# Four layers over a graph on one core: how layer 0 divides its keys, and a third buffer for turned blocks

## The chip, the cores and the metric

The kernel runs on one core of one Trainium2 chip. What counts is the device time of one execution in microseconds (us). A core has a matrix engine (PE, with a separate queue PEld that loads its weights), a vector engine (DVE), a scalar engine (ACT), GpSimd (POOL) and a queue that mainly issues transfers (SP). Each engine runs its own instructions in order, and waits on semaphores for the others. SBUF is the memory that the engines work in, PSUM holds what PE has computed, in banks of 128 partitions x 512 fp32 numbers.

## The reference

Four graph layers follow each other on 2,708 nodes with 512 features. Each adds its result to its input and normalises the rows. The change is in layer 0, attention of 8 heads with 64 features each:

```python
adj = jnp.maximum(adjacency_matrix, jnp.eye(n))
keys    = jnp.einsum('nj,hjk->hnk', node_matrix, Wks)
queries = jnp.einsum('nj,hjk->hnk', node_matrix, Wqs)
values  = jnp.einsum('nj,hjk->hnk', node_matrix, Wvs)
atts = jnp.einsum('hqk,hmk->hqm', queries, keys) / key_dim ** 0.5
atts = atts - 1e+16 * (1.0 - adj)[None, :, :]
atts = jax.nn.softmax(atts, axis=-1)
return jnp.einsum('hqm,hmk,hko->qo', atts, values, Wo)
...
x = _layernorm(x + _L0_gnn_ref(x, adj, ...))
x = _layernorm(x + _L1_gnn_ref(x, adj, ...))
x = _layernorm(x + _L2_gnn_ref(x, adj, ...))
x = _layernorm(x + _L3_gnn_ref(x, adj, ...))
```

So each head makes a 2708 x 2708 matrix of weights: scores, plus a mask from the adjacency matrix, exponentials of score minus row maximum, and their sums. All is in fp32.

## The kernel before

**Stages.** A first stage (0 to 216 us) computes keys (`KT`), queries (stored to DRAM) and values (`V`). The stage of the change (216 to about 1230 us) is the attention. Then come the output projection and layers 1 to 3, which the change does not touch.

**Pairs and rounds.** The 2,708 queries are 22 chunks of 128 rows (the last, `LAST`, has 20). Two heads are worked on together, so that a `Pair(c, p)` is chunk c with heads 2p and 2p+1; there are 21 x 4 of them, and one `Last` that holds all eight heads of the 20 rows: 85 in all. The loop at the end of the stage works on three pairs in each round: `new` gets its scores, `cur` (of the round before) has its weights turned, `late` (of two rounds before) is multiplied with the values. The order on PE, DVE and ACT is the order of the program, written out by hand (`manual_schedule`).

**What a round does.** For `new`, PE multiplies keys and queries into PSUM banks (L419, from a ring of 7 banks, `ps_s`), one bank for each head and part. DVE reads each bank, adds the mask, writes the score to the tile `s` in SBUF and keeps the maximum of the row (L441, followed by a short instruction that reads the accumulator). From the maxima DVE makes `nm` (L454). ACT then replaces scores by exponentials in place and keeps their sums (L460).

**Keys in two halves.** The 22 chunks of keys are divided into two halves: 0 to 10 (1,408 keys) and 11 to 21 (1,300 keys). Each half has its own tile `s` (tags `s0`, `s1`, two buffers each, `[128, 2 heads, keys]`) and is scored in three parts (`PARTS = 3`): 469, 469, 470 keys, then 433, 433, 434. ACT takes the exponentials of the first half at the end of the round (`weights(0)`) and those of the second half at the start of the next (`weights(1)`).

**Turning.** To multiply with the values, the weights must stand with the keys on the partitions. The first eight chunks of each half are *dealt* (`DEALT = 8`): DVE transposes blocks of 32 x 32 (`blocks`, L466) from `s` into a tile `d` (`dp`, 2 buffers of 1 MB), and four transfers of 256 KB (`deal`, L475, on SP's queue) move `d` into a tile `e` (`ep`, 3 buffers), which PE reads. The other six chunks (`turned`: 8, 9, 10, 19, 20, 21) are transposed whole by PE (L492) into three PSUM banks, which ACT copies to SBUF (L498, L495, L496). The second half of `cur` is transposed in one instruction for both heads, the first half of `new` in two, one for each head (`blocks(0, slice(j, j + 1))`), so that the first can start when the first head's exponentials are there. A `d` buffer is free again when the four transfers that read it have landed; with two buffers, the second half's blocks go to the buffer of the second half of the round before, and the first half's to that of the first half.

**The order of a round on each engine.**
- PE: scores of `new` (L419), values of `late` (L511), transposes of `cur` (L492).
- DVE: twelve instructions L441 of `new`, `nm` (L454), `blocks(1)` of `cur`, `blocks(0)` of `new` (L466).
- ACT: `weights(1)` of `cur` (L460), the preparation of the next chunk's mask, `weights(0)` of `new` (L460), the copy of the finished values (L529), the copies of the turned banks (L498, L495, L496).
- SP: the loads of the next chunk's adjacency rows (L177, L185), then the transfers L475 of `cur` and `new`.

**Preparing the mask.** In three of four rounds a third of the next chunk's adjacency rows (1,024, 1,024 or 660 columns) is prepared: ACT sums the row (`row_sums`, L195), DVE sets the diagonal where it lies in this third (`loops`, L209, in 20 rounds of the loop), ACT scales the rows to a mask (`mask`, L215). In the program `row_sums` stands after the scores of the first half, `loops` and `mask` after the first part of the second half. So DVE does L209 after eight of its twelve instructions L441.

Of the kernel before, what the change touches and what calls it, by code (L numbers as in the profile page):

```python
# [8 lines left out]
F32 = mybir.dt.float32  # L9
# [6 lines left out]
P = 128  # L16
# [6 lines left out]
def kernel(  # L23
# [27 lines left out]
    NC = (N + P - 1) // P  # L51
# [6 lines left out]
    def cols(b):  # L58
        return b * BLK, min(BLK, N - b * BLK)

    def chunks_of(b):
        n0, w = cols(b)
        return [n0 // P + i for i in range((w + P - 1) // P)]

    const = ctx.enter_context(tc.tile_pool(name="const", bufs=1))
    small = ctx.enter_context(tc.tile_pool(name="small", bufs=4))
# [51 lines left out]
    ends = [0, 8, 16, NC]  # L118
    KD4 = P // 32
    HALVES = 2  # L120
    PARTS = 3
    DEALT = 8
    bounds = [0, NC // 2, NC]

    def dealt(c):
        return any(a <= c < a + DEALT for a in bounds[:-1])
# [19 lines left out]
    with ExitStack() as l0:  # L146
# [40 lines left out]
        def row_sums(c, k):  # L187

            r0, q = rows(c)
            a = loaded[c][0]  # L190
            n0, w = batch(k)
            dst = dgp[:, c, k : k + 1]
            if c == LAST:
                q, dst = 32, dgz[:, k : k + 1]
            nc.scalar.activation(a[:q, n0 : n0 + w], a[:q, n0 : n0 + w], AF.Copy, accum_out=dst[:q])  # L195
            if c == LAST and k == NW - 1:
                nc.sync.dma_start(dgp[:LR, c, :], dgz[FILL:32, :])
# [13 lines left out]
        def mask(c, k):  # L211

            n0, w = batch(k)
            a = loaded[c][0][:, n0 : n0 + w]
            nc.scalar.activation(a, a, AF.Identity, scale=1e16, bias=far)  # L215

        with tc.tile_pool(name="kvw", bufs=1) as kvw, tc.tile_pool(name="xTb", bufs=2) as xtp, tc.tile_pool(
            name="ps_0", bufs=8, space=PSUM
# [63 lines left out]
            for b in order:  # L282
                n0, w = cols(b)
# [100 lines left out]
        ps_a = l0.enter_context(tc.tile_pool(name="ps_a", bufs=1, space=PSUM, reuse_waits="tile"))  # L384
        ps_s = l0.enter_context(tc.tile_pool(name="ps_s", bufs=7, space=PSUM, reuse_waits="tile"))
        sp = l0.enter_context(tc.tile_pool(name="sp", bufs=2, reuse_waits="tile"))
        dp = l0.enter_context(tc.tile_pool(name="dp", bufs=2, reuse_waits="tile"))
        ep = l0.enter_context(tc.tile_pool(name="ep", bufs=3, reuse_waits="tile"))
        ptp = l0.enter_context(tc.tile_pool(name="ptp", bufs=1, reuse_waits="tile"))

        def half(k):

            n0 = bounds[k] * P
            return n0, min(bounds[k + 1] * P, N) - n0

        def bank(shape, name):
            return ps_s.tile(shape, F32, tag="s", name=name)
# [3 lines left out]
        class Pair:  # L401


            def __init__(self, c, p):
                self.c, self.p = c, p
                self.s = []
                self.mx = small.tile([P, 2, HALVES * PARTS], F32, tag="mx", name=f"mx{c}_{p}")
                self.D = {}
                self.E = {}
                self.pts = {}  # L410
                self.done = 0
                self.av = None
# [15 lines left out]
            def scores(self, k, part):  # L428

                c, p = self.c, self.p  # L430
                a = loaded[c][0]
                n0, w = half(k)
                if part == 0:
                    self.s.append(sp.tile([P, 2, w], F32, tag=f"s{k}", name=f"s{c}_{p}_{k}"))
                s = self.s[k]
                h0, h1 = (w * i // PARTS for i in (part, part + 1))
                col = k * PARTS + part
                pss = [bank([P, BLK], f"pss{c}_{p}_{col}_{j}") for j in range(2)]
                self.products(pss, n0 + h0, h1 - h0)
                for j in range(2):  # L440
                    nc.vector.tensor_tensor_reduce(  # L441
                        out=s[:, j, h0:h1],
                        in0=pss[j][:, : h1 - h0],
                        in1=a[:, n0 + h0 : n0 + h1],
                        scale=1.0,
                        scalar=LOW,
                        op0=ALU.add,
                        op1=ALU.max,
                        accum_out=self.mx[:, j, col : col + 1],
                    )  # L450
# [8 lines left out]
                    s = self.s[k][:, j, :]  # L459
                    nc.scalar.activation(s, s, AF.Exp, bias=self.nm[:, j : j + 1], accum_out=self.sums(j, k))  # L460

            def blocks(self, k, heads=slice(0, 2)):

                if k not in self.D:
                    self.D[k] = dp.tile([P, KD4, 2, DEALT, 32], F32, tag="d", name=f"d{self.c}_{self.p}_{k}")
                nc.vector.transpose(  # L466
                    self.D[k].rearrange("p i j m x -> p j m i x")[:, heads],
                    self.s[k][:, heads, : DEALT * P].rearrange("p j (m i x) -> p j m i x", i=KD4, x=32),
                )

            def deal(self, k):
# [139 lines left out]
        with tc.manual_schedule(  # L611
            engines={mybir.EngineType.PE, mybir.EngineType.DVE, mybir.EngineType.Activation}
        ):
            for i in range(len(items) + 2):
                new = None
                more = i < len(items) and items[i][0] < LAST - 1
                prep = more and items[i][1] > 0
                if cur is not None:
                    cur.weights(1)
                if i < len(items):  # L620
                    c, p = items[i]
                    if more:
                        load_chunk(c + 1, p)
                    new = (Pair if c < LAST else Last)(c, p)
                    for part in range(PARTS):
                        new.scores(0, part)
                    if prep:
                        row_sums(c + 1, p - 1)
                    new.scores(1, 0)
                    if prep:  # L630
                        loops(c + 1, p - 1)
                        mask(c + 1, p - 1)
                    for part in range(1, PARTS):
                        new.scores(1, part)
                    new.maxima()
                    new.weights(0)
                if i in (HALF0 * NP + 2, len(items)):
                    sums = heads_sums(i == len(items))
                if late is not None:
                    late.values()  # L640
                if cur is not None:
                    cur.blocks(1)
                    cur.deal(1)
                if new is not None:
                    for j in range(2):
                        new.blocks(0, slice(j, j + 1))
                    new.deal(0)
                if cur is not None:
                    cur.turn()
                if i in (HALF0 * NP + 3, len(items) + 1):  # L650
                    heads_rows(*sums)
                if i == NP:
                    last_sums()
                late, cur = cur, new
# [83 lines left out]
    with tc.tile_pool(name="wo", bufs=1, reuse_waits="tile") as wop:  # L738
        wo_sb = wop.tile([P, KC, D], F32, tag="wo", name="wo_sb")
        load_rows(wo_sb, wo)  # L740
        for c in range(NC):
# [5 lines left out]
            heads = rz_d if c == LAST else rs_d[c >= HALF0][c % HALF0]  # L747
            heads = heads.rearrange("j p q -> j (p q)")
# [129 lines left out]
    if True:  # L878
# [115 lines left out]
        for b in range(NB):  # L994
            for m, _ in enumerate(graph1(b)):
# [6 lines left out]
                if b == NB - 2 and m in (3, 7, 11, 15):  # L1002
                    c = first[(m - 3) // 4]
                    top0(c, 0, piece(c, 0))
                if b == NB - 1 and m < len(first):
                    c = first[m]
# [79 lines left out]
    if True:  # L1086
# [53 lines left out]
        for b in range(NB):  # L1140
            if b:
                queue = Maxima(b + 1) if b + 1 < NB else None
            for m in graph2(b):
                if m % 4 == 2 and 0 <= m // 4 < len(chunks_of(b)) and b:
                    c = chunks_of(b)[m // 4]
# [25 lines left out]
    with tc.tile_pool(name="zp", bufs=2) as zp:  # L1171
# [87 lines left out]
        w = cols(TAIL)[1]  # L1259
# [22 lines left out]
        while n0 < NH * P:  # L1282
            w = min(BLK, NH * P - n0)
            n1 = NH * P + n0
            nchunks = w // P
            j = n0 // BLK
# [102 lines left out]
```

## Time and profile before

| what | value |
|---|---|
| time of three runs | 2588.0, 2579.19, 2587.2 us; median 2587.2 |
| the profiled execution | 2581.24 us; its span 2579.4 us, mean granted PE clock 0.993 |
| first stage, 0 to 216 us | PE busy 211.2, DVE 122.2, ACT 35.5 us |
| attention, 216 to 1230 us | PE busy 1002.5, DVE 967.2, ACT 745.7 us; DMA engines 77% busy, 214 GB/s |
| output projection, 1230 to 1400 us, with the start of layer 1 | PE busy 154.0, DVE 99.7 us |
| layers 1 to 3, 1400 to 2579 us | PE busy 1141.1, DVE 773.2, ACT 348.3 us |
| `nm` (L454), 85 times | first at 216.7 us, last at 1216.6 us |

The span runs from the first to the last instruction. An engine is busy while one of its instructions runs. The ends of PE's matmuls are modelled, so that a PE that is busy for 100% need not be at its limit. In the lines of instructions there stand the line of the program, the engine, the operation, output and input by the program's names, their shapes, how often, the busy time in us, the mean duration of one in ns, and after the last bar how long the engine stood idle just before them, with what ended that idle time.

### The profile page before, as it was taken

To read this page: it belongs to the slowest core of one execution; us is meant where nothing else is said; L and a number is where in the kernel's file an instruction comes from. 1 tells how busy PE (TensorE), PEld (TensorE's weight loads), DVE (VectorE), ACT (ScalarE), POOL (GpSimd) and SP (SyncE) were. 2 spreads that over 40 slices of the span, in tenths; PEclk is the share of its full clock that TensorE was granted. 3 is DMA by queue.
4 is the path that set the end of the run, shared out by engine and by line. 5 is a ranking of instruction groups with operands and counts; after the bars stand their busy time and mean duration, and the time that the engine had idled before them with its cause. 6 is when DMAs were issued, how large, how long until landed. Compare 5 with 4: busy or idle time off the path is not lost. (4 is left out here: it accounts for less than half of the span.)

```text
span 2579.4 us, 42415 instructions
## 1 busy us (share of the span) xinstructions
PE 2508.7 (97%) x15551; PEld 1558.2 (60%) x15551; DVE 1962.2 (76%) x4541; ACT 1154.0 (45%) x2070; POOL 315.7 (12%) x322
## 2 busy tenths in 40 slices
PE   9998999999999999999899999899999999999997
PEld 4886777777777777777456444444444465444465
DVE  3668999999999999999574777988776874543544
ACT  3104778777777777776011001565665640000000
POOL 2110000000000000000210000243332430000000
PEclk9999999999999999999999999999999999999999
DMA  5114787877877777877853444354433213644633
GB/s 167 62 50 138 218 226 211 240 213 220 230 210 219 218 211 215 225 204 186 236 169 94 126 121 142 118 158 138 125 109 116 64 31 114 184 141 143 178 103 105
DMA packets 221498, 411.43 MB, mean 160 GB/s; under 512 B 28765, under 2 KB 48911, under 8 KB 221292
## 3 DMA queue, kind: packets, MB, share of 16 engines
q1 hardware_dynamic: 215052, 392.00, 53.4%
q0 software_dynamic: 6240, 16.73, 1.9%
q8 instruction: 123, 2.02, 0.3%
q14 instruction: 83, 0.68, 0.1%
HBM read 213.55 MB, written 16.72 MB: 89 GB/s over the span
## 5 line engine op out<-in xcount | busy, mean ns | idle before, releaser
L460 ACT ACTIVATE s<-s,nm 128x1408 f32<-128x1408 f32 (+1 forms) x340 | 481.1, 1416 | 244.3 <-DVE nm L454 244.3
L441 DVE CUSTOM_DVE_ANT_0 s<-pss,adj 128x469 f32<-128x469 f32 (+2 forms) x1020 | 565.8, 622 | 8.2 <-PE pss L419 7.0
L419 PE MATMUL pss<-KT,qt 64*128 64x469 f32 (+2 forms) x2016 | 463.7, 561 | 7.2 <-DVE mx L441 4.6
L466 DVE STREAM_TRANSPOSE d<-s 128x1024 f32<-128x1024 f32 (+1 forms) x255 | 393.7, 1580 | 31.6 <-DMA e<-d 16.1
L419 PEld LDWEIGHTS pss<-KT,qt 64*128 64x128 f32 x2016 | 230.1, 187 | 200.3 <-issue 110.8
L811 PE MATMUL acc<-pt,x 128*128 128x512 f32 (+1 forms) x880 | 333.4, 537 | 12.2 <-ACT pt L864 9.7
L511 PE MATMUL av<-e,V 128*64 128x128 f32 x5376 | 309.6, 273 | 4.7 <-DMA e<-d 4.7
L511 PEld LDWEIGHTS av<-e,V 128*64 128x64 f32 x5376 | 297.8, 137 | 5.1 <-issue 5.1
L811 PEld LDWEIGHTS acc<-pt,x 128*128 128x128 f32 x880 | 157.2, 191 | 188.1 <-issue 162.2
L917 PE MATMUL acc<-at,h 128*128 128x512 f32 (+1 forms) x504 | 196.8, 543 | 0.0
L875 POOL TENSOR_TENSOR cs<-cs,pt 128x512 f32<-128x512 f32 (+2 forms) x110 | 157.3, 1430 | 202.7 <-ACT pt L864 200.4
L862 DVE TENSOR_TENSOR pt<-pt,at 128x512 f32<-128x512 f32 (+2 forms) x132 | 107.3, 820 | 75.6 <-ACT pt L861 75.4
L530 POOL DMA_DIRECT2D otd<-ot x84 | 45.2, 538 | 941.7 <-ACT ot L529 921.4
L94 ACT ACTIVATE ln_t<-lnve 128x1 f32<-128x1 f32 x88 | 17.7, 201 | 313.2 <-DVE lnve L108 313.1
L1251 ACT ACTIVATE z<-pz,rdeg 128x512 f32<-128x512 f32 (+1 forms) x22 | 15.1, 688 | 310.9 <-PE pz L823 310.9
L917 PEld LDWEIGHTS acc<-at,h 128*128 128x128 f32 x504 | 90.2, 190 | 101.4 <-issue 99.2
L492 PE MATMUL pst<-ident,s 128*128 128x128 f32 x1020 | 130.0, 277 | 0.0
L864 ACT ACTIVATE pt<-pt 128x512 f32<-128x512 f32 (+2 forms) x132 | 76.1, 579 | 110.0 <-DVE pt L863 109.8
L511 PEld LDWEIGHTS av<-pt,V 128*64 128x64 f32 x1680 | 90.0, 136 | 52.3 <-issue 51.5
L928 DVE SCALAR_TENSOR_TENSOR cs<-at,rdeg,cs 128x512 f32<-128x512 f32 (+2 forms) x126 | 86.2, 684 | 43.7 <-DMA at<-in_adjT_dram 42.4
L492 PEld LDWEIGHTS pst<-ident,s 128*128 128x128 f32 x1020 | 104.2, 133 | 16.8 <-issue 15.1
L511 PE MATMUL av<-pt,V 128*64 128x128 f32 x1680 | 110.3, 278 | 0.2 <-ACT pt L498 0.2
(348 smaller groups left out, 3474.5 us busy)
## 6 DMA issues: line engine op xcount, KB each, us to landing
e<-d SPq DMA_DIRECT2D x680, 256.0 KB
at<-in_adjT_dram SPq DMA_DIRECT2D x210, 256.0 KB
a<-in_adj_dram SPq DMA_DIRECT2D x38, 677.0 KB
adj<-in_adj_dram SPq DMA_DIRECT2D x42, 512.0 KB
at_a<-in_adjT_dram SPq DMA_DIRECT2D x40, 256.0 KB
at_c<-in_adjT_dram SPq DMA_DIRECT2D x40, 256.0 KB
at_f<-in_adjT_dram SPq DMA_DIRECT2D x40, 256.0 KB
adj<-in_adj_dram SPq DMA_DIRECT2D x21, 330.0 KB
```

The costliest lines, as they stand in the source:

```text
L419: nc.tensor.matmul(pss[j][:, :w], qt[h, self.p, :], KT[h, self.p, n0 : n0 + w], start=True, stop=True)
L441: nc.vector.tensor_tensor_reduce(out=s[:, j, h0:h1], in0=pss[j][:, : h1 - h0], in1=a[:, n0 + h0 : n0 + h1], scale=1.0, scalar=LOW, op0=ALU ...
L460: nc.scalar.activation(s, s, AF.Exp, bias=self.nm[:, j : j + 1], accum_out=self.sums(j, k))
L466: nc.vector.transpose(self.D[k].rearrange("p i j m x -> p j m i x")[:, heads], self.s[k][:, heads, : DEALT * P].rearrange("p j (m i x) -> ...
L492: nc.tensor.transpose(pt[:q, t, j, :], self.s[f][:, j, o : o + q], ident)
L511: nc.tensor.matmul(self.av[j * KD : (j + 1) * KD, out], V[:, m, h * KD : (h + 1) * KD], weights[j], start=(self.done == 0), stop=(self.don ...
L811: nc.tensor.matmul(acc[k][:, :w], last[0][g : g + mr, :] if m == NC - 1 else values[:mr, k * P : (k + 1) * P], moving[g : g + mr, :w], sta ...
L862: nc.vector.tensor_tensor(pt[:mr, :w], pt[:mr, :w], at[:mr, :w], ALU.subtract)
L864: nc.scalar.activation(pt[:mr, :w], pt[:mr, :w], AF.Exp)
L875: nc.gpsimd.tensor_tensor(sums[:mr, :w], sums[:mr, :w], pt[:mr, :w], ALU.add)
L917: nc.tensor.matmul(acc[hc][:, :w], lastH[g : g + mr, :] if m == NC - 1 else H[m][:mr, hc * P : (hc + 1) * P], at[g : g + mr, :w], start=(m ...
L928: nc.vector.scalar_tensor_tensor(sums[:mr, :w], at[:mr, :w], rdeg[:mr, m : m + 1], sums[:mr, :w], ALU.mult, ALU.add)
```

## The change

The keys are divided after 8 chunks instead of after 11: the first part has 1,024 keys, all of them dealt, the second 1,684, of which the first 1,024 are dealt and the other six chunks (16 to 21) turned by PE. The first part is scored in two parts of 512 keys, the second in four of 421. The tile of the first part gets one buffer (`bufs=k + 1`), that of the second two; a third buffer is given to `d`. `blocks(0)` becomes one instruction for both heads. The sizes of the `s` and `d` tiles add up to the same number of bytes as before. In the loop, `row_sums` now stands after two parts, `loops` and `mask` after the third.

```diff
-    PARTS = 3
+    PARTS = (2, 4)
     DEALT = 8
-    bounds = [0, NC // 2, NC]
+    bounds = [0, DEALT, NC]
...
-        dp = l0.enter_context(tc.tile_pool(name="dp", bufs=2, reuse_waits="tile"))
+        dp = l0.enter_context(tc.tile_pool(name="dp", bufs=3, reuse_waits="tile"))
...
-                    self.s.append(sp.tile([P, 2, w], F32, tag=f"s{k}", name=f"s{c}_{p}_{k}"))
+                    self.s.append(sp.tile([P, 2, w], F32, tag=f"s{k}", name=f"s{c}_{p}_{k}", bufs=k + 1))
                 s = self.s[k]
-                h0, h1 = (w * i // PARTS for i in (part, part + 1))
-                col = k * PARTS + part
+                h0, h1 = (w * i // PARTS[k] for i in (part, part + 1))
+                col = sum(PARTS[:k]) + part
...
-            def blocks(self, k, heads=slice(0, 2)):
-
-                if k not in self.D:
-                    self.D[k] = dp.tile([P, KD4, 2, DEALT, 32], F32, tag="d", name=f"d{self.c}_{self.p}_{k}")
+            def blocks(self, k):
+
+                self.D[k] = dp.tile([P, KD4, 2, DEALT, 32], F32, tag="d", name=f"d{self.c}_{self.p}_{k}")
                 nc.vector.transpose(
-                    self.D[k].rearrange("p i j m x -> p j m i x")[:, heads],
-                    self.s[k][:, heads, : DEALT * P].rearrange("p j (m i x) -> p j m i x", i=KD4, x=32),
+                    self.D[k].rearrange("p i j m x -> p j m i x"),
+                    self.s[k][:, :, : DEALT * P].rearrange("p j (m i x) -> p j m i x", i=KD4, x=32),
                 )
...
-                    for part in range(PARTS):
+                    for part in range(PARTS[0]):
                         new.scores(0, part)
                     if prep:
                         row_sums(c + 1, p - 1)
                     new.scores(1, 0)
                     if prep:
                         loops(c + 1, p - 1)
                         mask(c + 1, p - 1)
-                    for part in range(1, PARTS):
+                    for part in range(1, PARTS[1]):
                         new.scores(1, part)
...
                 if new is not None:
-                    for j in range(2):
-                        new.blocks(0, slice(j, j + 1))
+                    new.blocks(0)
                     new.deal(0)
```

More of the change, by code (lines that the diff above doesn't have):

```diff
@@ L406, in __init__ @@
                 self.s = []
-                self.mx = small.tile([P, 2, HALVES * PARTS], F32, tag="mx", name=f"mx{c}_{p}")
+                self.mx = small.tile([P, 2, sum(PARTS)], F32, tag="mx", name=f"mx{c}_{p}")
                 self.D = {}
```

## The prediction

> **What bounds the kernel now.** I read the page first, then busy time by stage, then who waits for whom in the attention, then the order of time in single rounds. On the page the costly groups of the attention are these:
>
> ```profile
> L460 ACT ACTIVATE s<-s,nm 128x1408 f32<-128x1408 f32 (+1 forms) x340 | 481.1, 1416 | 244.3 <-DVE nm L454 244.3
> L441 DVE CUSTOM_DVE_ANT_0 s<-pss,adj 128x469 f32<-128x469 f32 (+2 forms) x1020 | 565.8, 622 | 8.2 <-PE pss L419 7.0
> L466 DVE STREAM_TRANSPOSE d<-s 128x1024 f32<-128x1024 f32 (+1 forms) x255 | 393.7, 1580 | 31.6 <-DMA e<-d 16.1
> ```
>
> ACT waits 244 us for the maxima, so it has room. DVE stands idle for 8 us before the scores and 31.6 before the transposes, and in the attention it is busy for 967 of 1,014 us: DVE sets the pace, and its one large wait is L466's. PE is 1002 us "busy" there, so its room must be read from a round:
>
> ```profile
> 572.26 0.17 DVE L454 TENSOR_REDUCE nm<-mx 128x2 f32<-128x12 f32 x1
> 572.47 4.57 DVE L466 STREAM_TRANSPOSE d<-s 128x2048 f32<-128x2048 f32 x3
> 576.97 0.65 DVE L441 CUSTOM_DVE_ANT_0 s<-pss,adj 128x469 f32<-128x469 f32 x1
> ...
> 581.43 0.29 DVE L209 TENSOR_TENSOR adj<-adj,ident 128x128 f32<-128x128 f32 x1
> ...
> 583.87 0.17 DVE L454 TENSOR_REDUCE nm<-mx 128x2 f32<-128x12 f32 x1
> ```
>
> The reader sees a round without a wait (start, duration in us): the three transposes follow `nm` at once, the first score starts 4.71 us after `nm`, even 0.07 before the transposes end (572.47 + 4.57 = 577.04), and the next `nm` comes after 11.61, or some 11.4 where there is no L209 (0.2). The 84 rounds between the first and the last `nm` take 999.9 us, 11.90 each. The same round on ACT:
>
> ```profile
> 573.93 1.46 ACT L460 ACTIVATE s<-s,nm 128x1408 f32<-128x1408 f32 x1
> ...
> 576.75 0.36 ACT L496 COPY lastT<-pst 20x256 f32<-20x256 f32 x1
> 577.01 1.37 ACT L460 ACTIVATE s<-s,nm 128x1300 f32<-128x1300 f32 x1
> ...
> 579.75 1.04 ACT L195 ACTIVATE adj<-adj 128x1024 f32<-128x1024 f32 x1
> ```
>
> PE's transposes L492 start at 574.42, 2.16 after `nm`, and the next scores at 575.88, so a bank for DVE's first score is filled about half a us before DVE wants it. PE is close, but second.
>
> **What the change removes.** The wait for a `d` buffer. DVE's waits in order of size:
>
> ```profile
> DVE d L466 <- DMA e<-d: 16.1, 31, 1.5
> DVE s L441 <- PE pss L419: 7.0, 2, 5.7
> DVE d L466 <- ACT ot L529: 5.5, 6, 1.0
> DVE d L466 <- ACT pt L498: 3.3, 2, 1.9
> ```
>
> L466 reads neither `ot` nor `pt`, so lines 3 and 4 are the same wait for transfers, put down to whoever ended nearest. With three buffers `blocks(0)` takes the buffer of the *second* part of the round before, dealt some 2.3 us and four transfers earlier. In a stalled round (701 to 713 us) the DMA packets start 3.6 us after one `nm` and end 2.7 after the next, 10.9 us for both halves and the adjacency rows; the first of the two megabytes is through about 5 us earlier. The waits seen are at most 2 us, so I take them as gone. Bounds: all gone, or, if the transfers themselves are the limit, half (about 13 us) left. The DMA engines are 77% busy in this stage, which is nearer to the first.
>
> **What it adds on DVE's path in each round.** The transposes of both heads as one instruction wait for both exponentials; the first score has to wait for the transposes, since its tile has one buffer. The new chain, from `nm`:
> - to ACT's start: 0.20 (572.26, and 572.47 for L460).
> - two exponentials of 1,024. The second of a pair takes 1.46 for 1,408 and 1.36 for 1,300, 0.83 to 0.9 ns an element; 1,024 gives 1.12 to 1.15, two 2.27.
> - to the transposes' start: 0.13, from the first round, where they did wait for ACT:
>
> ```profile
> 219.78 0.19 ACT L460 ACTIVATION_READ_ACCUMULATOR s<-s,nm 128x1 f32 x1
> 219.87 1.36 ACT L460 ACTIVATE s<-s,nm 128x1300 f32<-128x1300 f32 x1
> 220.00 1.25 DVE L466 STREAM_TRANSPOSE d<-s 128x1024 f32<-128x1024 f32 x1 [0.21 <-ACT s L460]
> ```
>
> - the transposes: 2.31, the mean of the 2,048 form (the two of 1,024 take 2.25 to 2.33 together, so the merge itself gives nothing).
> - to the first score: 0.035. `nm` waits for DVE's own result before it and stands 2.9 us idle in 85 times, 0.034 each.
>
> Sum 4.945, against 4.66 to 4.71 in rounds without a wait: 0.15 for the second exponential, 0.11 for the lost overlap (0.07 to 0.08 plus 0.035). From the first score to `nm` nothing changes: twelve instructions for 2,708 keys and two heads as before, 6.67 to 6.70 us without L209. A round is 11.635.
>
> For the lost overlap the trace has the row above. Against it stands the Trainium skill, "VectorE: DVE Perf Modes", section "The DRAIN you can't avoid": a VectorE instruction starts only when the one before has left the pipeline, so a semaphore between them costs nothing extra. This trace shows an overlap of 0.07 us where nothing is waited for and a gap of 0.034 where something is, so I keep 0.11; by the rule the sum would be 84 x 0.11 = 9 us lower.
>
> **L209.** It moves from after eight scores to after six, while ACT, which must have summed the row, becomes later. ACT now: `weights(1)` starts 4.75 after `nm` (577.01). Exponentials before it are 0.66 shorter, but the copies of the turned banks then wait for PE (transposes end 3.69 after `nm`), so I take 0.35 of it: 4.40. Two exponentials of 1,684 at 1.70: 7.80. L195: 8.84, plus 0.13: 8.97. DVE is there at 4.945 + 3.47 (four scores of 512 at 0.61, two of 421 at 0.517, from the spacing 0.567 at 469 and 0.53 at 433) = 8.42. Wait 0.55 in the 15 rounds with 1,024 columns, 0.25 in the five with 660 (L195 then takes 0.74): 9.5 us. Bounds: 4 us (ACT the full 0.66 earlier) to 16 (not earlier at all). Behind L209 stand the six remaining scores and `nm`; `mask` still ends over 1.5 us before `nm`.
>
> **At no cost.** PE: the columns are the same, twelve matmul groups, twelve transposes; the bank that lets it begin the values is freed 0.13 later (the fifth score ends later), covered by its half us of room, which grows by 0.25; uncovered 84 x 0.13 = 11. Four more of the first stage's copies on POOL are rearranged (chunks 8 to 10 at 1.54 instead of 0.61, by the row of chunk 11): 2.8 us later, behind which DVE's L251 waits; 5 us stand before PE needs it, and DVE has a 3.9 us hole after; uncovered 2.8. SP issues as many transfers of the same sizes, in the same order. One buffer for the first tile holds up nobody else: only ACT and DVE touch it, and PE no longer transposes from it.
>
> **Sum.** 84 x 11.635 = 977.3; L209 itself 20 x 0.2 = 4.0; its waits 9.5; what stays: 7.0 for L441 in the first rounds, 0.8 for the sums of the heads, 1.6 for the degrees, 0.4 of small work there, 9.8. Together 1000.6, against 999.9: +0.7. At the end `blocks(1)` of the last pair waits 1.04 us for its buffer (1226.25); that goes, but the exponentials end 0.3 later: -0.7. So 2581.2 stays 2581. The four times shown (three runs and this one) have the mean 2583.9, the median of the runs is 2587.2; I name 2584.
>
> **Rivals.**
> - *The transfers set the pace* (slower). If the slowest DMA engine needs about the 11.6 us of a round, a third buffer only lengthens the queue, and waits of half the old 26 us or more stay: +13 to +27, 2597 to 2611. For it: in the stalled round single packets straggle for 1 us after the rest. Against: 77% busy, and a gap of some 1 us before the next packets even in the stalled round. It decides from a transfer work of 11.6 us a round; the stalled one has 10.9.
> - *The order on DVE costs nothing* (faster). If the exponentials come in time and the own wait is free, a round keeps 11.4: 84 x 0.25 = 21 less, with the L209 waits still there: 2560 to 2566. For it: the difference for the second exponential is only 0.15 us, worked out from a slope. Against: the rows of the first round and of `nm`.
> - *ACT takes DVE's place at L209* (slower). If ACT's start does not move and the copies wait longer, each of the 20 waits is 1 us or more: +11 and more, 2595 to 2600. ACT's 244 us of waiting speak against more.
>
> **How the numbers follow.** A measurement of this kernel tells about 0.5% (13 us) from no change. Cancelling terms: 0.60, its own range 2572 to 2598 (the bounds above and the 9 us between the runs). Transfers: 0.15. DVE order free: 0.17. L209: 0.08, half of it past 2600. From these, with a little of the first case's tails (0.01 faster, 0.03 slower), faster 0.18, same 0.60, slower 0.22. The range leaves out the far ends of the rivals: 2561 to 2606.
>
> **What would show it.** Waits of the transposes for `e<-d` near 0, and instead some 0.15 us for ACT before each `blocks(0)`, 13 us in all. `nm` to first score 4.9 to 5.0 in nearly every round, `nm` to `nm` 11.6. L209 waiting for L195, 4 to 16 us in sum. Wrong I am if transposes still wait for transfers, if the first score overlaps the transposes, or if L441 waits for PE.

## The result, and the profile after

The changed kernel takes 2601.0 us (median of 8 runs, 2587.6 to 2605.5), the kernel before 2586.5 us in the runs beside it. The ratio is 1.0062, with a 95% interval from 1.0041 to 1.0083: slower by 0.6%, some 15 us, where 2584 us and "no change" had been named. The profiled execution took 2600.91 us, its span is 2598.8 us with a mean granted PE clock of 0.988 (before: 2579.4 us and 0.993).

First, where the 19.4 us between the two spans lie. `nm` (L454) closes each of the 85 rounds, so its starts cut the span into four pieces:

| us | to the first `nm` | first to fifth `nm` | fifth to last `nm` (80 rounds) | from there to the end |
|---|---|---|---|---|
| before | 216.7 | 51.2 | 948.6 | 1362.9 |
| after | 218.2 | 63.7 | 956.3 | 1360.7 |
| difference | +1.5 | **+12.4** | **+7.6** | -2.1 |

More than half of the loss falls in four rounds out of 84. The rest is spread over the 80 rounds that follow. The groups on the page that answer to those of before:

```profile
L460 ACT ACTIVATE s<-s,nm 128x1024 f32<-128x1024 f32 (+1 forms) x340 | 480.9, 1415 | 251.0 <-DVE nm L454 251.0
L441 DVE CUSTOM_DVE_ANT_0 s<-pss,adj 128x421 f32<-128x421 f32 (+1 forms) x1020 | 567.8, 624 | 31.4 <-PE pss L419 17.9
...
L465 DVE STREAM_TRANSPOSE d<-s 128x2048 f32<-128x2048 f32 x170 | 392.6, 2310 | 14.9 <-ACT s L460 3.5
```

The work is what it was: the scores are busy for 567.8 us (565.8 before), the transposes for 392.6 (393.7). The idle time has moved: before the transposes it falls from 31.6 to 14.9 us, before the scores it rises from 8.2 to 31.4. DVE's waits in the attention, from the list of who waits for whom (in all, how often, the longest):

```profile
DVE s L441 <- PE pss L419: 17.9, 2, 16.5
DVE adj L209 <- ACT adj L195: 4.5, 13, 0.4
DVE d L465 <- ACT s L460: 3.5, 7, 2.4
```

The wait for `e<-d`, 16.1 us in 31 places before, is not in that list: the third buffer did what it should. In its place stands one single wait of 16.5 us for PE. Now a round without a large wait, on DVE (start, duration):

```profile
761.18 0.17 DVE L454 TENSOR_REDUCE nm<-mx 128x2 f32<-128x12 f32 x1
761.39 4.71 DVE L465 STREAM_TRANSPOSE d<-s 128x2048 f32<-128x2048 f32 x2
766.24 0.69 DVE L441 CUSTOM_DVE_ANT_0 s<-pss,adj 128x512 f32<-128x512 f32 x1
766.86 0.08 DVE L441 DVE_READ_ACCUMULATOR2_ANT mx<- 128x1 f32 x1
...
772.94 0.17 DVE L454 TENSOR_REDUCE nm<-mx 128x2 f32<-128x12 f32 x1
```

The transposes end at 761.39 + 4.71 = 766.10 and the first score starts at 766.24: a gap of 0.14 us, where before it started 0.07 us *before* their end. From `nm` to the first score it is 5.06 us (4.945 had been forecast), from `nm` to `nm` 11.76 (11.635). 58 of the 80 rounds take 11.8 when rounded to a tenth; before, the rounds without a wait took 11.3 to 11.6 and the others up to 13.4.

What sets the price of the gap stands in the trace's records of the queue. The score waits for two semaphores, one that PE sets (its bank) and DVE's own (the transposes). One of them stands on the instruction; the other is a separate semaphore instruction ahead of it, which runs 0.021 us at 766.13, 0.04 after the transposes; the score follows 0.08 after it. This gap of 0.14 us stands in nearly every round. `nm`, whose only wait stands on the instruction itself, starts 0.034 after what it waits for.

The 80 rounds can be summed from the same view of groups, limited to the stretch from the fifth `nm` to the last. First before, then after:

```profile
L441 DVE CUSTOM_DVE_ANT_0 s<-pss,adj 128x469 f32<-128x469 f32 (+2 forms) x960 | 532.5, 622 | 1.3 <-PE pss L419 1.3
L466 DVE STREAM_TRANSPOSE d<-s 128x1024 f32<-128x1024 f32 (+1 forms) x240 | 370.6, 1580 | 28.6 <-DMA e<-d 15.1 <-ACT ot L529 5.5 <-ACT pt L498 3.3
```

```profile
L441 DVE CUSTOM_DVE_ANT_0 s<-pss,adj 128x421 f32<-128x421 f32 (+1 forms) x960 | 534.4, 624 | 13.2 <-PE pss L419 1.4 <-DVE d L465 0.5
L465 DVE STREAM_TRANSPOSE d<-s 128x2048 f32<-128x2048 f32 x160 | 369.5, 2311 | 11.7 <-ACT s L460 0.8 <-issue 0.4
...
L209 DVE TENSOR_TENSOR adj<-adj,ident 128x128 f32<-128x128 f32 x19 | 5.5, 292 | 4.7 <-ACT adj L195 4.5
```

Idle time before the transposes: -16.9 us (of the 11.7 that remain, 8.7 are gaps of about 0.1 before the second transpose of a round, which now waits for the second exponential). Before the scores: +11.9. Before L209: +4.7. To this comes the overlap that is gone, 0.07 to 0.08 at the end of the transposes and 0.03 in the first score, whose start no longer falls into that end (first score to `nm`: 6.700 us, 6.668 before): some 0.1 in each of 80 rounds, about 8 us. Together about +8, and 7.6 is what the two `nm` show. So the change gave 16.9 us here, and took back more.

**The first rounds** are another matter. Two views show it: busy time by stretch, and the order of time on PE. By stretch, before and after (the columns: stretch, length, busy time and number of instructions of each engine, granted clock, share of the DMA engines, GB/s):

```profile
216.00:235.00 19.00, 12.60 (x48) 7.30 (x47) 17.05 (x44) 12.70 (x19) 0.00 (x0) 0.85 0.62 170
235.00:263.00 28.00, 28.00 (x511) 22.50 (x510) 22.16 (x56) 18.69 (x36) 1.26 (x2) 0.98 0.55 147
```

```profile
216.00:235.00 19.00, 12.99 (x50) 6.96 (x46) 15.99 (x39) 10.53 (x17) 0.00 (x0) 0.82 0.57 153
235.00:263.00 28.00, 27.25 (x379) 24.43 (x380) 11.66 (x28) 9.77 (x20) 0.71 (x1) 0.51 0.37 95
```

From 235 to 263 us PE is busy all the time in both, but after, it gets through 379 matmuls instead of 511, at a granted clock of 0.51 instead of 0.98, and DVE is busy for 11.7 of the 28 us. In the order of time, PE before, the values of `Last` for one of its four pairs of heads (20-column matmuls):

```profile
221.85 4.22 PE L419 MATMUL pss<-KT,qt 64*128 64x433 f32 x10 [4.13 <-DVE mx L441]
...
236.92 0.77 PE L511 MATMUL avz<-pt,V 128*64 128x20 f32 x20
237.52 0.28 PE L511 MATMUL avz<-lastT,V 128*64 128x20 f32 x4
237.64 2.03 PE L511 MATMUL avz<-e,V 128*64 128x20 f32 x64
```

and after:

```profile
224.00 2.47 PE L419 MATMUL pss<-KT,qt 64*128 64x421 f32 x5 [4.82 <-DVE mx L441]
...
240.33 1.26 PE L510 MATMUL avz<-pt,V 128*64 128x20 f32 x20
241.42 0.39 PE L510 MATMUL avz<-lastT,V 128*64 128x20 f32 x4
241.63 3.59 PE L510 MATMUL avz<-e,V 128*64 128x20 f32 x64
```

PE's idle time in the second round (in square brackets) grows from 4.13 to 4.82 us, since the first round's transposes now wait for two exponentials (2.44 us; 1.68 before). The clock is at half for 6.8 us from 221.5, then for 27.3 us without a break from 235.2 to 262.5 (before: 3.4 us twice, at 222.4 and 232.6). The values of the four pairs, 10.4 us before, take 18.9 us. Only then does PE go on to the scores of the next round, for which DVE has been waiting:

```profile
242.15 4.74 DVE L465 STREAM_TRANSPOSE d<-s 128x2048 f32<-128x2048 f32 x2
263.38 0.69 DVE L441 CUSTOM_DVE_ANT_0 s<-pss,adj 128x512 f32<-128x512 f32 x1 [16.49 <-PE pss L419]
```

Before, this wait was 5.65 us. The 10.8 us of difference are nearly all of the 12.4 of these rounds.

### The profile page after: what moved, and what is told of

Read it like the earlier page. It is cut to its first block, busy times and chain, and to the rows that moved or that the text cites. A ratio compares the mean times of both kernels' runs of the same rounds, so it can differ in the third digit from the quotient of the medians.

```text
span 2598.8 us, 42438 instructions
## 1 busy us (share of the span) xinstructions
PE 2530.5 (97%) x15551; PEld 1568.2 (60%) x15551; DVE 1967.7 (76%) x4456; ACT 1161.2 (45%) x2070; POOL 316.5 (12%) x322
## 4 chain that ended last, share of the span: by engine, by line
issue 49%; PE 39%; DVE 4%; POOL 2%; DMA 2%; ACT 1%; SPq 1%; POOLq 0%; ACTq 0%; DVEq 0%
PE acc L809 12%; PE acc L915 7%; PE m L1219 5%; PE pf L821 2%; PE psk L261 2%; POOL otd L529 2%; PE ph L901 1%; PE psv L261 1%; PE psq L261 1%; PE p L946 1%; PE po L755 1%; PE pz L821 1%; PE psv L357 1%; DMA otl<-otd 1%; PE psq L309 1%
## 5 line engine op out<-in xcount | busy, mean ns | idle before, releaser
L460 ACT ACTIVATE s<-s,nm 128x1024 f32<-128x1024 f32 (+1 forms) x340 | 480.9, 1415 | 251.0 <-DVE nm L454 251.0
L441 DVE CUSTOM_DVE_ANT_0 s<-pss,adj 128x421 f32<-128x421 f32 (+1 forms) x1020 | 567.8, 624 | 31.4 <-PE pss L419 17.9
L419 PE MATMUL pss<-KT,qt 64*128 64x421 f32 (+1 forms) x2016 | 474.2, 566 | 7.0 <-DVE mx L441 5.8
L465 DVE STREAM_TRANSPOSE d<-s 128x2048 f32<-128x2048 f32 x170 | 392.6, 2310 | 14.9 <-ACT s L460 3.5
L809 PE MATMUL acc<-pt,x 128*128 128x512 f32 (+1 forms) x880 | 333.4, 537 | 11.9 <-ACT pt L862 9.7
L491 PEld LDWEIGHTS pst<-ident,s 128*128 128x128 f32 x1020 | 106.0, 134 | 17.1 <-issue 15.5
```

The source lines that it names most:

```text
L419: nc.tensor.matmul(pss[j][:, :w], qt[h, self.p, :], KT[h, self.p, n0 : n0 + w], start=True, stop=True)
L441: nc.vector.tensor_tensor_reduce(out=s[:, j, h0:h1], in0=pss[j][:, : h1 - h0], in1=a[:, n0 + h0 : n0 + h1], scale=1.0, scalar=LOW, op0=ALU ...
L465: nc.vector.transpose(self.D[k].rearrange("p i j m x -> p j m i x"), self.s[k][:, :, : DEALT * P].rearrange("p j (m i x) -> p j m i x", i= ...
L491: nc.tensor.transpose(pt[:q, t, j, :], self.s[f][:, j, o : o + q], ident)
L809: nc.tensor.matmul(acc[k][:, :w], last[0][g : g + mr, :] if m == NC - 1 else values[:mr, k * P : (k + 1) * P], moving[g : g + mr, :w], sta ...
```

## The experiments

Three causes are to be told apart: the cold start (PE's clock), the own wait before the first score, the second exponential. One thing is to be priced: the third buffer. Times are given as ratios to the kernel before, in runs beside it.

**The changed kernel once more.** No edit; it asks whether the first rounds are the same in each execution.

> The changed kernel once more, unchanged, for a second trace of it. Open is whether the clock's fall in the first rounds is in every execution, and how much of the time between executions lies elsewhere. Theory (the fall follows from the order of the work): granted clock at half for 20 us and more between 218 and 290 us again, first four rounds 61 to 66 us, 80 rounds 955 to 957.5, and what differs from the first trace lies behind the attention (1358 to 1370 us). Rival (the fall was a chance of that one execution): first four rounds under 58 us, and the mean clock of most of the runs at 0.991 or more.

2601.8 us (6 runs), ratio 1.0063 [1.0046, 1.0081]. The clock is at half from 221.1 for 6.8 us and from 234.7 for 27.3 us; the first four rounds take 63.6 us, the 80 rounds 956.2, the rest 1361.8. So the cold start was no chance of one execution. Whether it is in each of them can be told by the mean granted clock alone, which is on record for every run: 13 of the 14 runs of this kernel have 0.983 to 0.989; one, of 2587.6 us, has 0.992, like the kernel before (0.988 to 0.993), and probably had no cold start.

**Two buffers for `d` again.**

```diff
-        dp = l0.enter_context(tc.tile_pool(name="dp", bufs=3, reuse_waits="tile"))
+        dp = l0.enter_context(tc.tile_pool(name="dp", bufs=2, reuse_waits="tile"))
```

> The changed kernel with two buffers for turned blocks instead of three. Theory (the third buffer does its work, and the loss comes from elsewhere): the transposes wait for e<-d again, less than before the change because blocks(0) now starts 2.6 us after nm instead of 2.44 and a round is 11.8 instead of 11.4 us long: 5 to 20 us of such waits, and the time 5 to 20 us above the changed kernel. Rival (the third buffer is worth nothing in this order, since everything is now later than the transfers): under 2 us of waits and the same time.

2611.3 us, ratio 1.0090 [1.0059, 1.0121]. The wait is back:

```profile
DVE s L441 <- PE pss L419: 18.1, 2, 16.7
DVE d L465 <- DMA e<-d: 12.5, 16, 1.5
DVE d L465 <- ACT pt L497: 3.5, 3, 1.2
```

The 80 rounds take 968.7 us, 12.5 more than with three buffers. The rest of this execution is long as well (1368.0 us), as it is in a trace below with three buffers, so that this is no matter of the buffer. The third buffer is worth 12.5 us in this order. That is less than the 26 us of waits that it had been credited with. Rounds that the other additions make some 0.35 us longer (11.76 against 11.4) leave the transfers more time, which would explain it; this was not tested apart.

**The blocks of the first part by head again.**

```diff
-                    new.blocks(0)
+                    for j in range(2):
+                        new.blocks(0, slice(j, j + 1))
```

(with `blocks` taking `heads` as before the change)

> The changed kernel with blocks(0) again as two instructions, one for each head. Theory (DVE waits for the second exponential): the waits of the transposes for ACT go, nm to the first score falls from 5.06 to 5.13 us to about 4.9, some 0.15 to 0.2 us in each of 84 rounds, 12 to 17 us less. Rival (one instruction in place of two saves at least what it waits): the same time or up to 5 us more.

2584.4 us (10 runs), ratio 0.9998 [0.9983, 1.0014]: as fast as before. `nm` to first score is 4.915 (5.064), the 80 rounds take 947.0 us, 9.3 less, although L209 now waits 7.7 us instead of 4.7. The gap of 0.14 before the first score is still there (12.5 us before the scores), so it is no matter of the second exponential. The start changed too: 56.1 us for the first four rounds, with the clock at half for 6.8 and 10.2 us. The one merged instruction thus costs the kernel twice: 0.15 us in each round, and a longer start. How it makes the start longer is not settled: PE's idle time in the second round is 3.75 us here, shorter than before the change (4.13), and the clock falls in it all the same.

**The second part's tile scored first.** It has two buffers, so that nothing written there waits for the transposes just issued. The edit also moves `loops` and `mask` back to after eight scores.

```diff
-                    for part in range(PARTS[0]):
-                        new.scores(0, part)
+                    for part in range(3):
+                        new.scores(1, part)
                     if prep:
                         row_sums(c + 1, p - 1)
-                    new.scores(1, 0)
+                    new.scores(1, 3)
                     if prep:
                         loops(c + 1, p - 1)
                         mask(c + 1, p - 1)
-                    for part in range(1, PARTS[1]):
-                        new.scores(1, part)
+                    for part in range(PARTS[0]):
+                        new.scores(0, part)
```

> The changed kernel with the four parts of the second tile (two buffers) scored first, then the two of the first tile (one buffer); loops and mask after four parts. Theory (the first score waits for DVE's own transposes, 0.144 us idle and 0.07 of overlap lost): the gap before the first score goes, nm to the first score falls by 0.2 us in each round, 17 us, and the 4.5 us of L209's waits go too: 18 to 22 us less. Rival (the gap is the engine's own pause after a transpose, a semaphore costs nothing): the gap stays, only L209's 4.5 us go.

2568.0 us (6 runs), ratio 0.9941 [0.9920, 0.9962]: faster than both. The same round in its order of time:

```profile
757.24 0.17 DVE L454 TENSOR_REDUCE nm<-mx 128x2 f32<-128x12 f32 x1
757.45 4.77 DVE L465 STREAM_TRANSPOSE d<-s 128x2048 f32<-128x2048 f32 x2
762.14 0.56 DVE L441 CUSTOM_DVE_ANT_0 s<-pss,adj 128x421 f32<-128x421 f32 x1
762.63 0.08 DVE L441 DVE_READ_ACCUMULATOR2_ANT mx<- 128x1 f32 x1
```

The score starts 0.08 us before the transposes end (757.45 + 4.77 = 762.22), and the next one 0.49 later. The idle time before the scores falls from 13.2 to 1.3 us in the 80 rounds; `nm` to first score is 4.844 (5.064), first score to `nm` 6.669 (6.700). That is 0.25 us a round, 20 us in 80 rounds; with the 4.7 us of L209, whose wait is gone as well, 24.7 of the 26.5 that the 80 rounds gain (929.8). A wait for DVE's own result on the chain costs 0.25 us here, not 0.11. That is the price of the wait and not of the second semaphore: the first score has a separate semaphore instruction here too, at 759.93, but what it waits for is long done, and it runs while the transposes do. The gain is above the 18 to 22 us expected. The start is as cold as in the changed kernel (64.1 us, the clock at half for 6.8 and 30.7 us), so that this cause stands apart from the first one.

**The diagonal after eight scores, as before the change.** One run.

```diff
-                    new.scores(1, 0)
+                    for part in range(2):
+                        new.scores(1, part)
                     if prep:
                         loops(c + 1, p - 1)
                         mask(c + 1, p - 1)
-                    for part in range(1, PARTS[1]):
+                    for part in range(2, PARTS[1]):
```

> The changed kernel with loops and mask one part later, after eight of the twelve scores as in the kernel before. Theory (L209 comes too early for ACT's row sums): its 4.7 us of waits go and nothing takes their place; the 80 rounds from the fifth nm to the last fall from 956.3 to about 951.5 us. Rival (ACT is late anyway, the wait moves on to nm or to the exponentials): the 80 rounds stay within 2 us of 956.3.

No wait before L209, and 951.5 us for the 80 rounds, 4.7 less; the whole time of the single run, 2599.4 us, tells nothing at this size. The wait was all that the earlier place cost.

**PE kept busy in the first rounds.** Unread matmuls are added where PE idles, 36 in the second round and 12 in the third; nothing else changes.

```diff
+                    if i in KEEP:
+                        idle = ps_a.tile([P, P], F32, tag="av", name=f"idle{i}")
+                        for _ in range(KEEP[i]):
+                            nc.tensor.matmul(idle, ident, ident, start=True, stop=True)
                     for part in range(1, PARTS[1]):
```

> The changed kernel with matrix multiplications that nobody reads in PE's idle time of the first rounds: 36 in the second round, 12 in the third. Theory (PE idles at the start, its granted clock falls to 0.5 for 27 us, and the values of Last run at half speed): the clock stays at 1.0 from 228 to 270 us, the values of Last take 10.4 us instead of 19, DVE's wait of 16.5 us for the scores becomes about 5.7, and the time falls by 9 to 12 us; the later rounds stay at 11.76. Rival (DVE waits there because its first rounds are longer, whatever the clock): the wait stays above 14 us and the time is the same or up to 5 us more.

2591.4 us (10 runs), ratio 1.0042 [1.0027, 1.0058]: by the ratio some 5 us less than the changed kernel, where 9 to 12 had been expected. At the start the clock is at half for 3.4 us only (235.0 to 238.4), the values of the four pairs take 10.4 us, DVE waits 9.7 us for PE in all (17.9 without the added work), the first four rounds take 55.7 us and the 80 rounds 956.3, unchanged. The added matmuls run for 8.3 us where the idle time was 4.8, so they delay the start themselves.

**The same, sized to the idle time** (16 and 5, each two records of about 0.12 us).

> The changed kernel with unread multiplications that are sized to PE's idle time: 16 in the second round and 5 in the third, each two records of 0.115 us (as the run with 36 and 12 showed: 8.30 us for 36), so 3.7 and 1.2 us. Theory (the clock falls because PE idles 4.8 us and then stays at half for the 20-column products): the first four rounds take 51 to 53.5 us (63.7 in the changed kernel, 55.7 with 36 and 12), the 80 rounds stay at 956, the time is 2586 to 2591. Rival (3.7 us of a single 128-row product is not enough to hold the clock, the longer stretch was needed): the clock falls to half at 235 us again, first four rounds over 58 us.

PE in the second round, and the stretch of the values:

```profile
218.62 3.84 PE L636 MATMUL idle<-ident 128*128 128x128 f32 x32
222.39 0.97 PE L419 MATMUL pss<-KT,qt 64*128 64x421 f32 x2
224.03 2.45 PE L419 MATMUL pss<-KT,qt 64*128 64x421 f32 x7 [0.67 <-DVE mx L441]
```

```profile
235.00:263.00 28.00, 28.00 (x511) 22.78 (x511) 22.38 (x55) 18.43 (x35) 1.27 (x2) 1.00 0.56 150
```

With 3.8 us of added work in the gap the clock never falls; the stretch has 511 matmuls, as before. The first four rounds take 52.4 us, 11.3 less than without, and the 80 rounds 956.3. So the cold start comes from PE's idle times in the second and third rounds, and 11 us is its price there. Which of the two idle times counts was not separated, since both runs fill both. The expectation for the whole time (2586 to 2591) was missed all the same: 2596.5 us (4 runs), ratio 1.0056 [1.0035, 1.0076]. In the trace the rest after the last `nm` is 1368.0 us, 7.3 more than in the changed kernel; the clock is at half there for 34.1 us, in stretches of 3.4 to 10.2, against 20.5. The section on the hardware comes back to this.

**The kernel before, with such matmuls** (32 and 14, then 16 and 7): is there something to gain without the change?

> The kernel before the change with the same kind of unread matrix multiplications in PE's idle time: 32 in the second round, 14 in the third. Theory (the clock at the start costs the kernel before something too, 3 to 8 us, and a different amount from run to run): no half clock between 222 and 240 us, the first four rounds fall from 51.2 to 46 to 50 us, and the times lie 2 to 8 us below the median before, closer together. Rival (only the changed kernel falls into the slow clock): the same time.

> The kernel before with 16 and 7 unread multiplications (3.7 and 1.6 us, where PE idles 4.1 and 2.3). Theory (what the start can give is the few us that the clock is at half, 3.4 us twice): first four rounds 46 to 51 us (51.2 without), the 80 rounds 948 to 949, the time within 0.3% of before, 2579 to 2588. Rival (any added work in the chain costs more than the clock gives back, as 32 and 14 did): over 54 us.

With 32 and 14: 2588.6 us (10 runs), ratio 1.0024 [1.0008, 1.0039]. The first expectation was missed: the added work is longer than the idle time (7.4 and 5.4 us against 4.1 and 2.3), the first four rounds rise to 57.0 us, and the clock falls all the same, for 6.8 us at 232. With 16 and 7: 2582.9 us (10 runs), ratio 0.9999 [0.9985, 1.0013], the first four rounds at 53.3, outside the 46 to 51 expected. In the kernel before, these two runs found no cold start worth removing.

**Together: second tile first, blocks by head, unread matmuls** (36 and 12).

> The changed kernel with the second tile scored first, blocks(0) by head, loops after four parts and the unread matrix multiplications. Theory (these are the added terms, and DVE still sets the pace): nm to the first score 4.66 to 4.71 us, rounds of 11.36, the 80 rounds from the fifth nm to the last 912 to 920 us, the time 2540 to 2553 us, 1.2 to 1.8% below the kernel before. Rival (PE takes over below 11.6 us a round): L441 waits for PE in most rounds, the 80 rounds stay above 925 us and the time above 2558.

2558.6 us (6 runs), ratio 0.9909 [0.9892, 0.9927]. The 80 rounds take 922.5 us, 11.33 to 11.37 in 56 of them, and miss the 912 to 920 of the theory, as the time misses its 2540 to 2553. PE's waits for transfers in these rounds, of which the changed kernel has none:

```profile
PE av L511 <- DMA e<-d: 3.2, 4, 1.1
```

In four rounds PE waits 0.6 to 1.1 us for a transfer before it can multiply with the values, and in a fifth 2.0 us for something that the view doesn't name; DVE waits behind these for its scores, 4.8 us in all. Behind the last `nm` PE waits for transfers as well (3.1 and 1.4 us), but so it does in the kernel before (2.5 and 2.2). At rounds of 11.4 us the transfers begin to show.

**The same with 16 and 6 unread matmuls, and with none.**

> Second part's tile scored first, the blocks of the first part by head, loops after four parts, and 16 and 6 unread multiplications (3.7 and 1.4 us) in place of 36 and 12. Theory: first four rounds 51 to 54 us (57.3 with 36 and 12), 80 rounds 920 to 924, time 2551 to 2556. Rival (the clock is not held by the shorter stretch): first four rounds over 58, time 2559 and more.

> The same without any unread multiplication, so that its price and gain can be read beside the run above. Theory (PE idles 4 to 5 us in the second round, the clock falls to half while the 20-column products run): first four rounds 56 to 64 us, 80 rounds 920 to 924, time 2556 to 2566. Rival (by-head blocks let the values begin earlier, and the start stays warm): under 54 us, and no gain from the run above.

With 16 and 6: 2551.3 us (4 runs), ratio 0.9881 [0.9863, 0.9899]; 52.8 us for the first four rounds, 918.2 for the 80 (920 to 924 had been expected). With none: 2550.2 us (4 runs), ratio 0.9888 [0.9867, 0.9910]. In the trace the latter's start is colder (17.1 us at half, first four rounds 55.4, 80 rounds 921.5), but its profiled execution is the slowest of its four. Both numbers of the theory for it (56 to 64 us, 2556 to 2566) are missed by a little at the start and by more in the time. The two cannot be told apart by their times: after the other two edits, the unread work is not worth keeping. The version with the two edits alone is 1.1% faster than the kernel before.

What was not tried: the third buffer on the kernel before alone, and a second buffer for the first part's tile beside it. Each takes 8 KB a partition more than the kernels here.

## Why the prediction was wrong

- *The wait for `d`*: right. 26 us had been taken as gone; in the changed kernel the trace puts no gap above 0.04 us down to `e<-d` in the 80 rounds, and under 2 us in all. "The transfers set the pace" fell for this kernel; the two-buffer run, with 12.5 us, shows that the buffer was needed. Only when the rounds came down to 11.4 us did waits for transfers show, a little and at PE instead of DVE.
- *The second exponential*: right. 0.15 us a round had been forecast; going back to blocks by head gives 0.149.
- *"To the first score: 0.035"*: **this term failed.** The price was taken from `nm`, whose wait stands on the instruction. The score already waits for PE, DVE's own semaphore stands as an instruction of its own in the queue, and the gap is 0.144. Lost overlap and own wait had been put at 0.11 a round; taking the wait away gave 0.25. A plain round is 11.764 us instead of 11.635, 10.3 us in 80 rounds. The rival that put this wait at nothing was further off still. So was the rule weighed there, from the Trainium skill, "VectorE: DVE Perf Modes", section "The DRAIN you can't avoid", by which the semaphore costs nothing extra: the traces show 0.144 us of gap where it is waited for, and an overlap of 0.08 where it isn't. The same section says that an instruction that is not held starts earlier, which the prediction left out, and with which the overlap agrees.
- *From the first score to `nm`, 6.67 to 6.70*: right, 6.70.
- *L209*: 9.5 us had been forecast, with 4 to 16 as bounds; 4.7 was measured, 13 waits of up to 0.4. ACT starts the second part's exponentials 4.44 us after `nm` in the round shown (765.62), much as taken (4.40); DVE comes 0.12 us later than taken, which is over half of what the waits fall short (0.35 instead of 0.55). The rival that made ACT the limit fell.
- *"What stays: 7.0 for L441 in the first rounds"*, and *PE "at no cost"*: **this step failed, and it weighs most.** The columns and the groups were counted, and they are the same; that the same matmuls would run at half the clock was not looked at, though the profile of before already showed the clock falling twice there. DVE waits 17.9 us for PE in place of the 7.0, and L441 waiting for PE had been named as a sign of being wrong. By the runs with unread matmuls these 10.9 us come from PE's idle times; the run with blocks by head shows that the merged instruction has a part in it. That it works through the 0.7 us by which PE's idle time in the second round is longer is not shown.
- *The first stage "at no cost"*: the first `nm` comes 1.5 us later, within the 2.8 named for the case that it was not covered; the other traces with the new division of the keys have 0.2 to 2.0.

The sum, with what was measured put in place: 84 x 11.764 = 988.2 for the rounds; L209 itself 4.0; its waits 4.7; what stays, 20.7 instead of 9.8, with 17.9 for L441. That gives 1017.6 us between the first and the last `nm`, where 1000.6 had been forecast and the trace shows 1019.9; the 2.3 us left were not followed up. The two failed steps are of nearly equal size (10.8 and 10.9 us) and both of the same sign, while the forecast had let losses and gains of some 26 us cancel to a microsecond: a sum of that kind is only as good as its smallest term times 84.

What stays open: by the traces the cold start costs 11 us in the first rounds, but the runs without it are better by only 0.06 to 0.2% in their ratio (1.0056 and 1.0042, against 1.0062 and 1.0063, with intervals of 0.2% each way). The granted clock of the runs without a trace tells a part of it. The 34 us at half clock at the start are worth 0.0066 of the mean. With 36 and 12 the ten runs have 0.992 to 0.996, on average 0.0063 more than the changed kernel: there the cold start seems gone in all of them, but the added work itself delays the start. With 16 and 5 the four runs have 0.990 to 0.992, only 0.0037 more: about half of what is gained at the start is lost at other places, as in the trace, where the clock is at half for longer behind the attention.

## What to carry to other kernels

A wait for a result just made, added to an instruction that waits already, has its own price (0.144 us here, and the overlap besides): look in the trace for an instruction with the same waits, and don't take that of an instruction with one. A tile with a single buffer on the engine that sets the pace should be written last in a round and not first; that was worth 1.2% here, L209's wait included. And where the matrix engine idles for some microseconds ahead of dense small matmuls, price these at half the clock too.

## What the runs showed of the hardware

**A clock that small matmuls did not bring back.** In all fourteen traces of this case the stretches of half clock, but for the last one at the kernel's end, are multiples of 3.41 us. Where the clock is at half when the 20-column matmuls of `Last` begin (240.33 in the changed kernel), it stays there as long as they run, 27.3 to 30.7 us in five traces, and comes back 2 to 6 us after their end; where it had come back before they began (236.0, with the matmuls from 236.92, in the kernel before), they ran at full clock. It can also fall within them: in the two traces with blocks by head and no added work it falls at about 246 us, amid these matmuls, for 10.2 us. The Trainium skill, "TensorE: Matmul & The Clock Gate", section "Part 1: The HAM clock gate (the "warmup" mystery)", gives a window of about 3.4 us, in which an idle PE loses half its clock and a busy one gets it back. The stretches here agree with the window's length. The loss did not need a whole idle window: in the 3.4 us before the long fall at 235.2 the trace has PE idle for 1.3 us. That one busy window restores the clock does not agree: for 18.9 us, over five such windows, PE had matmuls of 20 columns without a pause, and the clock stayed at half. What the gate counts as busy was not settled.

**The end of the kernel scatters with the same windows.** From the last `nm` to the end every kernel here does nearly the same work. It took 1358.0 us in the trace with 13.7 us of half clock there (without the last stretch at the kernel's end), and 1368.0 in those with 34.1 and 37.5. The 20.4 us at half clock between the first two of these are worth 10.2 at full speed, the size of the difference; no run changed these stretches alone. A gain of a few microseconds at the start can be hidden by it.

**Where transfers begin to limit.** With three buffers, rounds of 11.76 us show no wait for `e<-d` above 0.04 us; rounds of 11.36 show 3.2 us at PE, in four of 80 rounds (0.5 and 1.5 us in the two later traces at this pace).
